# Projection weights as a float32r and a scaled float16 part in a fused attention block on one core

## The chip, the cores and the metric

The kernel runs on one core of one Trainium2 chip. The metric is the device time of one execution in microseconds (us), as the median of several runs. TensorE (PE) multiplies matrices into PSUM, VectorE (DVE) and ScalarE (ACT) read PSUM and SBUF, GpSimd (POOL) works on SBUF alone, SyncE (SP) issues most DMAs. Each engine takes its instructions in the order in which the program queued them.

## The reference

x has the shape (4, 512, 48, 48), so 4 batches, 512 channels and T = 2304 positions; 8 heads of 64 channels.

```python
hn = group_norm(x)                                  # 32 groups
qkv = einsum('oc,bchw->bohw', qkv_w, hn) + qkv_b    # float32, then cast to float16
w = softmax(einsum('bhct,bhcs->bhts', q * scale, k * scale))
a = einsum('bhts,bhcs->bhct', w, v).astype(float32) # a float16 result, widened
out = einsum('oc,bchw->bohw', proj_w, a) + proj_b
return x + out
```

The change concerns the last two lines: the projection of a with proj_w in float32, the bias proj_b, and the residual x.

## The kernel before

The program runs fast_path, which ends in a flag; if a test of its own has failed (a sum of exponentials out of range), general_path computes everything again.

fast_path goes through 16 pairs of heads (4 batches with 4 pairs each), and within a pair through 5 blocks of queries (four of 512 columns, one of 256). The work of a block is a stream of steps, three key tiles of two heads at a time: scores (L1066) on PE into one of three PSUM buffers, exponentials (L1073) on ACT into one of three p tiles, an add of that p tile to a running sum acc (L1122) on DVE, and the product with v (L1091) on PE into the only av buffer. At the end of a block, two joins (L1127) fold acc, a copy empties av (L1100), ones are multiplied with acc for the sums of the rows (L1150, also in the av buffer), and the sums go through SBUF and DRAM to be inverted and spread over partitions. GpSimd then writes the block's quotient to att in float16 (L1215).

Between the scores and the values of a step, fill (L1460) adds other work to PE's queue by a plan with fixed estimates of its cost: chains of matmuls for later pairs' q and k (L802) and v (L854), and the projection of the batch before. All these chains use one PSUM bank, ps_w, with a single buffer, so that a chain waits until the one before has been evacuated: q and k by L813, v by L862, the projection by L975, all on DVE. do_tasks adds statistics (L624) and normalization (L756) of the next batch on DVE.

The projection: the float16 result att of each pair is converted to float32r tiles at32 (att32, L940 on GpSimd and L942 on ACT). The weights of each of four channel chunks c are loaded during pair 0 and split (split_wproj, L566): whi is the weight rounded to float32r (L568), wlo the remainder, also in float32r (L569). proj_chain (L944) multiplies both parts with at32 and accumulates them: for each 128 output channels and 512 columns eight matmuls, in the order whi, wlo of c = 0, whi, wlo of c = 1 and so on. The evacuation (L975) adds the bias and the residual tile r in one operation; r, a part of x, is loaded two chains ahead (residual, L905). Batch 0 is projected during batch 1, batch 1 during batch 2, batch 2 and part of batch 3 during batch 3; for the last blocks of batch 3 the chain is cut in FIRST (three pairs, with the bias) and LAST (the fourth pair, L971, without it). In the tail `beyond` lets ACT copy a bank (L1592) and GpSimd add it to r.

fine (L593) holds the results of check_sums, which multiplies the outcome of each range test into it; at the end it is counted along with the tests of the last block (L1621 to L1644).

split_wproj is queued by put_run in pair 0, once for each chunk, between chains for q and k of pair 1.

Of the kernel before, what the change touches and what calls it, by code (L numbers as in the profile page):

```python
# [12 lines left out]
F32 = mybir.dt.float32  # L13
F32R = mybir.dt.float32r
F16 = mybir.dt.float16
I32 = mybir.dt.int32
AF = mybir.ActivationFunctionType
ALU = mybir.AluOpType
AX = mybir.AxisListType
# [3 lines left out]
B, C, T = 4, 512, 48 * 48  # L23
# [3 lines left out]
P = 128  # L27
NC = C // P
NPAIR = HEADS // 2
# [13 lines left out]
QB = 512  # L43
QBLOCKS = [(o, min(QB, T - o)) for o in range(0, T, QB)]
# [2 lines left out]


SUM_MIN, SUM_MAX = 256.0, 60000.0


IDLE = {"sync": 62, "scalar": 27, "gpsimd": 64, "tensor": 190}
# [418 lines left out]
def fast_path(  # L471
# [12 lines left out]
    nc = tc.nc  # L484

    RES = NC
    const = ctx.enter_context(tc.tile_pool(name="const", bufs=1))
# [37 lines left out]
    bproj = const.tile([P, NC], F32, name="bproj")  # L525
# [29 lines left out]


    whi = const.tile([P, NC, C], F32R, name="whi")
    wlo = const.tile([P, NC, C], F32R, name="wlo")

    wproj = {}  # L560

# [3 lines left out]

    def split_wproj(c):  # L566
        w = wproj.pop(c)
        nc.vector.tensor_copy(whi[:, c, :], w)  # L568
        nc.vector.tensor_tensor(  # L569
            wlo[:, c, :], w, whi[:, c, :].bitcast(F32), ALU.subtract  # L570
        )

    mhalf = const.tile([P, 2], F32, name="mhalf")
    nc.gpsimd.memset(mhalf, -0.5)
# [15 lines left out]
            channel_multiplier=sign,  # L590
        )

    fine = const.tile([P, 2 * QB // P], F32, name="fine")  # L593
    nc.gpsimd.memset(fine, 1.0)

# [2 lines left out]
    def chain_bank(name):  # L600
        if alone[0]:
            return ps_s.tile([P, 2, QB], F32, tag="ps", name=name)[:, 0, :]
        return ps_w.tile([P, QB], F32, tag="pw", name=name)
# [275 lines left out]
    atts, res, at32 = {}, {}, {}  # L879
# [9 lines left out]
    def rows_of(dram_tensor, b, j, chunks):  # L889
        o, n = QBLOCKS[j]  # L890
        found = dram_tensor[b, chunks[0] * P : (chunks[-1] + 1) * P, o : o + n]
        return found.rearrange("(m p) n -> p m n", p=P)
# [50 lines left out]

    def proj_chain(b, j, m, ps, pairs=range(NC)):  # L944
        n = QBLOCKS[j][1]
        steps = [(c, w) for c in pairs for w in (whi, wlo)]
        for i, (c, w) in enumerate(steps):
            nc.tensor.matmul(  # L948
                ps[:, :n],
                w[:, c, bass.ts(m, P)],  # L950
                at32[b, j, c],
                start=(i == 0),
                stop=(i == len(steps) - 1),
            )

    FIRST, LAST = range(NC - 1), range(NC - 1, NC)

    def proj_run(b, j, chunks, pairs=range(NC), bank=None):

        n = QBLOCKS[j][1]  # L960
        if bank is None:
            bank = chain_bank(f"pr_{b}_{j}_{chunks[0]}")
        places = [bank[:, i * n : (i + 1) * n] for i in range(len(chunks))]
        for m, ps in zip(chunks, places):
            proj_chain(b, j, m, ps, pairs)
        xt = res[b, j, chunks[0]]

        def evacuate():
            if pairs == LAST:
                ps = bank[:, : len(chunks) * n].rearrange("p (m n) -> p m n", n=n)  # L970
                nc.vector.tensor_tensor(xt, ps, xt, ALU.add)  # L971
            else:
                for i, m in enumerate(chunks):
                    bias = bproj[:, m : m + 1]
                    nc.vector.scalar_tensor_tensor(  # L975
                        xt[:, i], places[i], bias, xt[:, i], ALU.add, ALU.add
                    )

        def store(engine=nc.sync):
            engine.dma_start(rows_of(out, b, j, chunks), xt)  # L980

        return evacuate, store

    def proj_piece(b, j, chunks, pairs=range(NC), ahead=None):
        def run():
            evacuate, store = proj_run(b, j, chunks, pairs)
            evacuate()
            if pairs == LAST:
                finished.add((j, chunks[0]))

            if pairs != FIRST:
                loads.append((now[0] + 1, store))
            if ahead is not None:
                loads.append((now[0] + 1, ahead))

        return piece(QB / 290.0 * len(pairs) / NC, run, True, True)
# [320 lines left out]
    for b in range(B):  # L1317
        g = b * NPAIR
        old = b - 1
        if b == 0:  # L1320
            for j in range(NQ):
                if j < NC:
                    put_run(load_wproj, j)
                if j > 0:
                    put_run(split_wproj, j - 1)
                put_qk(g + 1, 1, (j,))
                put_qk(g + 1, 0, (j,))
            for block in SPARE:
                put_run(reload, *block)
# [183 lines left out]
    for n in range(end):  # L1513
# [34 lines left out]
        if n - BEHIND in soon:  # L1548
            g, j = stream[n - BEHIND][:2]
# [9 lines left out]
    g, b, j = NG - 1, B - 1, NQ - 1  # L1559
    n = QBLOCKS[j][1]  # L1560
# [21 lines left out]
    def last_run(k, bank=None):  # L1582
        return proj_run(b, *k, LAST, bank)

    def beyond(k, name, tag):
        bank = chain_bank(name)
        _, store = last_run(k, bank)
        t = xpool.tile([P, QB], F32, tag=tag, name=f"beyond_{name}")
        xt = res[b, k[0], k[1][0]].rearrange("p m n -> p (m n)")

        def copy():
            nc.scalar.copy(t, bank)  # L1592

        def finish():
            nc.gpsimd.tensor_tensor(xt, t, xt, ALU.add)  # L1595
            return store

        return copy, finish
# [4 lines left out]
    o = QBLOCKS[j][0]  # L1603
# [14 lines left out]
        copy, later = beyond(ahead[1], "ahead_1", "x1_3")  # L1618
        copy()

    every = fine.shape[1] + n  # L1621
    fines = work.tile([P, QB], F32, tag="rows", name="fines")[:, :every]
    nc.gpsimd.tensor_scalar(fines[:, :n], inv, 1.0 / SUM_MAX, None, ALU.is_ge)  # L1623
    ok = work.tile([P, QB], F32, tag="avx", name="ok")[:, :n]
    nc.gpsimd.tensor_scalar(ok, inv, 1.0 / SUM_MIN, None, ALU.is_le)  # L1625
    nc.gpsimd.tensor_tensor(fines[:, :n], fines[:, :n], ok, ALU.mult)  # L1626
    nc.gpsimd.tensor_copy(fines[:, n:], fine)  # L1627
    if len(ahead) > 1:
        store_ahead = later()

# [16 lines left out]
@with_exitstack  # L1647
def group_norm_attention(ctx: ExitStack, tc: tile.TileContext, *args):
    nc = tc.nc
    keep = ctx.enter_context(tc.tile_pool(name="keep", bufs=1))  # L1650
    flag = keep.tile([1, 1], I32, name="flag")

    kinds = mybir.EngineType
    engines = {kinds.PE, kinds.DVE, kinds.Pool, kinds.SP, kinds.Activation}
    with tc.manual_schedule(engines=engines):
        fast_path(tc, flag, *args)
    fails = nc.values_load(
        flag[0:1, 0:1],
        min_val=0,
        max_val=1,  # L1660
        skip_runtime_bounds_check_because="it is the result of a comparison",
    )
    with tc.If(fails > 0, label="fallback"):
        general_path(tc, *args)
# [37 lines left out]
```

## Time and profile before

| | us |
|---|---|
| median of 3 runs | 1597.47 |
| lowest and highest | 1597.33, 1597.59 |
| span of the profiled execution | 1595.6 |
| the runs' median less that span | 1.9 |

For the profiled execution the span, from its first to its last instruction, is the only time there is. A row of a group names the line, the engine, the operation, what it writes and reads with shapes, how often it ran, the busy us and the mean ns of one, and how long the engine was idle just before. A row of the timeline begins with its start and its length in us; "x6" merges six instructions of a kind. A row of windows has the length of the stretch, each engine's busy us with the number of instructions, the granted clock of TensorE, the share of DMA and GB/s. PE's matmuls are pipelined and their ends are modelled, so the distance from start to start says more than the length of one. PEld is the load of weights, which runs beside the matmul before it.

### The profile page before, as it was taken

Reading aid. Unit: us, or ns where it says so; the run is one execution under the profiler, and the core shown is the slowest. Engines: PE = TensorE matmul, PEld = TensorE weight load, DVE = VectorE, ACT = ScalarE, POOL = GpSimd, SP = SyncE. Lnnn points to the kernel's source line nnn. Section 1 sums busy time; section 2 is a strip of 40 time slices with the busy share of each in tenths; the row PEclk is TensorE's granted clock in tenths of the full one; section 3 lists DMA queues with packets and bytes.
Section 4 is the critical chain, followed back from the end, with each engine's and each line's share of the span. In section 5 each row is a group of like instructions: output and inputs, shape, how many; then the busy total and the mean of one; then the engine's idle time right before and its main releaser. Section 6 shows DMA issues by size and latency. Waiting matters only on the chain. (4 is left out here: it accounts for less than half of the span.)

```text
span 1595.6 us, 28731 instructions
## 1 busy us (share of the span) xinstructions
PE 1582.0 (99%) x11526; PEld 701.7 (44%) x11526; DVE 1140.2 (71%) x1302; ACT 1269.4 (80%) x1363; POOL 336.8 (21%) x463
## 2 busy tenths in 40 slices
PE   9999999999999999999999999999999999999997
PEld 3733434443333534545333354455533334434554
DVE  6267668876666678887666666888767676767776
ACT  4177777888888888888888888887878888888885
POOL 1001202222121222312112121222212121121232
PEclk9999999999999999999999999999999999999999
DMA  7002020000000024521000001353101000015424
GB/s 222 3 14 67 12 73 16 18 14 12 15 18 11 12 69 119 144 67 28 11 14 18 14 12 41 111 158 88 23 17 18 15 15 11 15 31 166 149 62 133
DMA packets 94896, 82.10 MB, mean 51 GB/s; under 512 B 50852, under 2 KB 60964, under 8 KB 94756
## 3 DMA queue, kind: packets, MB, share of 16 engines
q1 hardware_dynamic: 92724, 78.35, 18.1%
q8 instruction: 92, 1.51, 0.4%
q10 hardware_dynamic: 1904, 1.84, 0.4%
q14 instruction: 48, 0.39, 0.1%
q0 software_dynamic: 128, 0.01, 0.0%
HBM read 60.70 MB, written 19.17 MB: 50 GB/s over the span
## 5 line engine op out<-in xcount | busy, mean ns | idle before, releaser
L1073 ACT ACTIVATE p<-ps 128x1024 f16<-128x1024 f32 x1296 | 1233.5, 1025 | 299.1 <-PE ps L1066 296.3
L1122 DVE TENSOR_TENSOR acc<-acc,p 128x3072 f16<-128x3072 f16 x270 | 485.4, 1798 | 53.8 <-ACT p L1073 51.3
L802 PE MATMUL pqk<-x,wqkv 128*64 128x512 f32 (+1 forms) x2432 | 510.3, 549 | 0.1
L1091 PE MATMUL av<-p,v 128*64 128x512 f16 (+1 forms) x2880 | 360.6, 364 | 0.0
L1066 PE MATMUL ps<-q,k 64*128 64x512 f16 (+1 forms) x2880 | 355.8, 358 | 0.4 <-DVE v L862 0.2
L854 PE MATMUL pv<-wqkv,x 128*64 128x256 f32 x2304 | 267.6, 379 | 0.3 <-DVE v L862 0.3
L802 PEld LDWEIGHTS pqk<-x,wqkv 128*64 128x64 f32 x2432 | 168.5, 137 | 205.4 <-issue 155.9
L1188 POOL TENSOR_SCALAR in<-sums 128x8 f32<-128x8 f32 (+1 forms) x158 | 100.8, 638 | 712.4 <-DMA sums<-slx 705.8
L1066 PEld LDWEIGHTS <-k 64*128 64x128 f16 x2880 | 105.9, 94 | 287.2 <-issue 238.2
L1091 PEld LDWEIGHTS <-v 128*64 128x64 f16 x2880 | 131.2, 109 | 212.8 <-issue 168.1
L1215 POOL TENSOR_TENSOR att<-avx,ib 128x512 f16<-128x512 f32 (+1 forms) x78 | 133.1, 1706 | 422.9 <-DMA ib<-row 373.7
L854 PEld LDWEIGHTS pv<-wqkv,x 128*64 128x64 f32 x2304 | 166.3, 137 | 81.3 <-DVE v L862 0.8
L1122 DVE TENSOR_TENSOR acc<-p,p 128x3072 f16<-128x3072 f16 x79 | 138.1, 1748 | 0.0
L948 PE MATMUL pr<-a,whi 128*128 128x512 f32 (+1 forms) x311 | 121.8, 399 | 0.1
L1127 DVE TENSOR_TENSOR acc<-acc 128x1024 f16<-128x1024 f16 x156 | 114.7, 735 | 3.3
L948 PE MATMUL pr<-a,wlo 128*128 128x512 f32 (+1 forms) x311 | 113.5, 372 | 0.0
L813 DVE TENSOR_SCALAR q<-pqk,bqkv 128x512 f16<-128x512 f32 (+1 forms) x77 | 53.5, 694 | 76.0 <-PE pqk L802 75.5
L813 DVE TENSOR_SCALAR k<-pqk,bqkv 128x512 f16<-128x512 f32 (+1 forms) x75 | 52.2, 695 | 77.7 <-PE pqk L802 77.5
L862 DVE TENSOR_TENSOR v<-pv,bv 128x512 f16<-128x512 f32 x72 | 49.7, 690 | 79.6 <-PE pv L854 79.5
L1166 DVE COPY slx<-sl 128x512 f32<-128x512 f32 (+1 forms) x79 | 50.6, 641 | 64.1 <-PE sl L1150 64.1
L975 DVE SCALAR_TENSOR_TENSOR r<-pr,bproj,r 128x512 f32<-128x512 f32 (+1 forms) x80 | 54.9, 695 | 41.3 <-PE pr L948 36.6
L1100 DVE COPY avx<-av 128x512 f32<-128x512 f32 (+1 forms) x79 | 50.6, 640 | 36.4 <-PE av L1091 36.1
(124 smaller groups left out, 506.7 us busy)
## 6 DMA issues: line engine op xcount, KB each, us to landing
r<-x_dram SPq DMA_DIRECT2D x72, 256.0 KB, 3.6
out_dram<-r SPq DMA_DIRECT2D x69, 256.0 KB, 2.4
ib<-row SPq DMA_DIRECT2D x126, 128.0 KB, 3.1
x<-x_dram SPq DMA_DIRECT2D x62, 256.0 KB, 3.9
x<-x_dram SPq DMA_DIRECT2D x16, 128.0 KB, 4.8
sums<-slx SPq DMA_DIRECT2D x128, 2.0 KB, 2.1
ib<-row SPq DMA_DIRECT2D x30, 64.0 KB, 3.0
wqkv<-qkv_wT_dram SPq DMA_DIRECT2D x2, 768.0 KB, 6.9
```

The costliest lines, as they stand in the source:

```text
L802: nc.tensor.matmul(pw[0][lo : lo + D, :n], wqkv[:, c, w0 + lo : w0 + lo + D], hn[b, c, j], start=(c == 0), stop=(c == NC - 1),)
L813: nc.vector.tensor_scalar(qk[g][part][:, o : o + n], pw[0][:, :n], bqkv[:, col : col + 1], SCALE, ALU.add, ALU.mult,)
L854: nc.tensor.matmul(pw[0][lo : lo + D, a, :], hn[b, c, i * P // QB][:, at + lo : at + lo + D], wqkv[:, c, 2 * C + half * C // 2 :][:, : C / ...
L948: nc.tensor.matmul(ps[:, :n], w[:, c, bass.ts(m, P)], at32[b, j, c], start=(i == 0), stop=(i == len(steps) - 1),)
L975: nc.vector.scalar_tensor_tensor(xt[:, i], places[i], bias, xt[:, i], ALU.add, ALU.add)
L1066: nc.tensor.matmul(ps[:, h, a * n : (a + 1) * n], kt[rows, bass.ts(i, P)], qt[rows, o : o + n], start=True, stop=True,)
L1073: nc.scalar.activation(pt[:, r], ps, AF.Exp)
L1091: nc.tensor.matmul(av[0][lo : lo + D, :n], vv[b, pr // 2][:, i, pr % 2 * P + lo : pr % 2 * P + lo + D], pt[:, r, h, a * n : (a + 1) * n], ...
L1122: nc.vector.tensor_tensor(t, before, pt, ALU.add)
L1127: nc.vector.tensor_tensor(t[:, 0], t[:, 0], t[:, r], ALU.add)
L1188: nc.gpsimd.tensor_scalar(t, sm, limit, None, op)
L1215: nc.gpsimd.tensor_tensor(atts[g][:, o : o + n], avx.pop((g, j))[:, :n], ibs.pop((g, j))[:, :n], ALU.mult,)
```

## The change

The weight is scaled by 2^26 when it is split. whi is the scaled weight rounded to float32r; the remainder is cast to float16 as wlo, and whether that cast was exact is tested on the chip: GpSimd subtracts wlo from the remainder and compares with zero, DVE takes the minimum into split_ok, four new columns of the tile that held fine. At the end these are counted with the other tests. In a chain, wlo comes ahead of whi and multiplies att itself, in float16; whi multiplies at32 as before. The scale is taken out at the evacuation (DOWN). The bias is no longer added there but to the residual tile, in operations of its own that are queued ahead of the chain.

```diff
+UP = 2.0**26
+DOWN = 1.0 / UP
...
-    wlo = const.tile([P, NC, C], F32R, name="wlo")
+    wlo = const.tile([P, NC, C], F16, name="wlo")
...
     def split_wproj(c):
         w = wproj.pop(c)
-        nc.vector.tensor_copy(whi[:, c, :], w)
-        nc.vector.tensor_tensor(
-            wlo[:, c, :], w, whi[:, c, :].bitcast(F32), ALU.subtract
+        nc.vector.tensor_scalar(whi[:, c, :], w, UP, None, ALU.mult)
+        nc.vector.scalar_tensor_tensor(
+            w, w, UP, whi[:, c, :].bitcast(F32), ALU.mult, ALU.subtract
         )
+        nc.vector.tensor_copy(wlo[:, c, :], w)
+        nc.gpsimd.tensor_tensor(w, w, wlo[:, c, :], ALU.subtract)
+        nc.gpsimd.tensor_scalar(w, w, 0.0, None, ALU.is_equal)
+        nc.vector.tensor_reduce(split_ok[:, c : c + 1], w, AX.X, ALU.min)
...
-    fine = const.tile([P, 2 * QB // P], F32, name="fine")
-    nc.gpsimd.memset(fine, 1.0)
+    tests = const.tile([P, 2 * QB // P + NC], F32, name="tests")
+    nc.gpsimd.memset(tests, 1.0)
+    fine, split_ok = tests[:, : 2 * QB // P], tests[:, 2 * QB // P :]
...
     def proj_chain(b, j, m, ps, pairs=range(NC)):
         n = QBLOCKS[j][1]
-        steps = [(c, w) for c in pairs for w in (whi, wlo)]
-        for i, (c, w) in enumerate(steps):
+        o = QBLOCKS[j][0]
+        steps = [
+            s
+            for c in pairs
+            for s in (
+                (wlo[:, c], atts[b * NPAIR + c][:, o : o + n]),
+                (whi[:, c], at32[b, j, c]),
+            )
+        ]
+        for i, (w, a) in enumerate(steps):
             nc.tensor.matmul(
                 ps[:, :n],
-                w[:, c, bass.ts(m, P)],
-                at32[b, j, c],
+                w[:, bass.ts(m, P)],
+                a,
...
+        xt = res[b, j, chunks[0]]
+        if pairs != LAST:
+            for i, m in enumerate(chunks):
+                nc.vector.tensor_scalar(
+                    xt[:, i], xt[:, i], bproj[:, m : m + 1], None, ALU.add
+                )
         for m, ps in zip(chunks, places):
             proj_chain(b, j, m, ps, pairs)
-        xt = res[b, j, chunks[0]]

         def evacuate():
-            if pairs == LAST:
-                ps = bank[:, : len(chunks) * n].rearrange("p (m n) -> p m n", n=n)
-                nc.vector.tensor_tensor(xt, ps, xt, ALU.add)
-            else:
-                for i, m in enumerate(chunks):
-                    bias = bproj[:, m : m + 1]
-                    nc.vector.scalar_tensor_tensor(
-                        xt[:, i], places[i], bias, xt[:, i], ALU.add, ALU.add
-                    )
+            ps = bank[:, : len(chunks) * n].rearrange("p (m n) -> p m n", n=n)
+            nc.vector.scalar_tensor_tensor(xt, ps, DOWN, xt, ALU.mult, ALU.add)
...
-            nc.scalar.copy(t, bank)
+            nc.scalar.mul(t, bank, DOWN)
...
-    every = fine.shape[1] + n
+    every = tests.shape[1] + n
...
-    nc.gpsimd.tensor_copy(fines[:, n:], fine)
+    nc.gpsimd.tensor_copy(fines[:, n:], tests)
```

## The prediction

> **What bounds the kernel now.** I read the engines' line of the page first, then the groups by shape, then busy time by window for the stretches that hold projection work, and last the timeline around the lines the change touches.
>
> ```profile
> span 1595.6 us, 28731 instructions
> PE 1582.0 (99%) x11526; PEld 701.7 (44%) x11526; DVE 1140.2 (71%) x1302; ACT 1269.4 (80%) x1363; POOL 336.8 (21%) x463
> ```
> TensorE (PE) has work for 99% of the span, so time saved on it is time saved, and any wait put in front of it is time lost. The other engines have slack on average. The average hides three stretches in which the projection chains of batches 0, 1 and 2 run:
>
> ```profile
> 628.90:686.00 57.10, 57.10 (x356) 32.10 (x356) 51.55 (x74) 47.97 (x56) 19.03 (x23) 1.00 0.56 158
> 1035.50:1092.20 56.70, 56.70 (x316) 30.10 (x314) 50.94 (x71) 48.38 (x57) 12.16 (x18) 1.00 0.56 161
> 1445.40:1502.00 56.60, 56.60 (x353) 32.04 (x352) 40.55 (x44) 49.95 (x61) 16.84 (x25) 1.00 0.65 198
> ```
> Columns: length, then busy us of PE, weight loads, VectorE (DVE), ACT, POOL. In the first two VectorE is busy for 51.55 of 57.10 and 50.94 of 56.70 us (90%), because it also normalizes the next batch there; in the third for 40.55 (72%).
>
> **Saving on TensorE.** Each 512-wide chain is eight matmuls (four pairs of whi and wlo). One chain:
>
> ```profile
> 629.03 0.50 PE L948 MATMUL pr<-a,whi 128*128 128x512 f32 x1
> 629.36 0.39 PE L948 MATMUL pr<-a,wlo 128*128 128x512 f32 x1
> ...
> 630.76 0.39 PE L948 MATMUL pr<-a,wlo 128*128 128x512 f32 x1
> 631.08 0.82 PE L1066 MATMUL ps<-q,k 64*128 64x512 f16 x6
> ```
> From the second to the eighth start, 629.36 to 630.76 us, six steps take 1.40 us: 0.233 us each. The first step takes 0.33 us: the first weight load of a chain isn't hidden. The groups show it over all chains:
>
> ```profile
> L948 PE MATMUL pr<-a,whi 128*128 128x512 f32 x251 | 106.4, 424 | 0.1
> L948 PE MATMUL pr<-a,wlo 128*128 128x512 f32 x251 | 99.0, 394 | 0.0
> ```
> (106.4 - 99.0) = 7.4 us is what the open first loads cost in the 512-wide chains. The change does two things here. It puts wlo first, with float16 weights, and it runs half the matmuls with float16 on both sides. The rows nearest to that are the warm-up matmuls, float16 with 128x128 weights and 512 columns:
>
> ```profile
> 1.52 4.95 PE L1405 MATMUL idle<-busy 128*128 128x512 f16 x16 [1.52 <-DVE busy L1401]
> 8.85 1.02 PE L1405 MATMUL idle_again<-busy 128*128 128x512 f16 x4
> L1405 PEld LDWEIGHTS <-busy x20: 95/98/181, 1.5 to 9.3; 128*128 128x128 f16 x20
> L948 PEld LDWEIGHTS pr<-a,wlo x311: 187/188/192, 629.1 to 1577.7; 128*128 128x128 f32 x156
> ```
> Four take 1.02 us, of which the last one's own duration is 0.38: 0.64 over three steps, 0.214 us a step against 0.233. So a wlo matmul saves 0.019 us; for the 251 of the group 4.8 us. The float16 load takes 98 ns against 188: 90 ns of the 100 ns that the first load leaves open go, 0.9 x 7.4 = 6.7 us. Together 11.5 us; the half-width chains may add up to 1 us (estimate, half the columns and fewer of them). If the load saves nothing, 4.8 us stay; that is the low end. The Trainium skill, page "TensorE: Matmul & The Clock Gate", section on weight-path perf modes, says that 128 weights that aren't FP32 are read in four parallel chunks, and its load formula gives 107 ns for 128 columns; by these, as an estimate, the saving per chain would be 80 ns instead of 90 and the sum of first loads 6 us. The traced loads go the same way, and I keep the rows.
>
> Of the 11.5 us, each of the first two windows holds 16 chains of 64 + 64 matmuls: 64 x 0.019 + 16 x 0.09 = 2.7 us. That leaves 11.5 - 5.4 = 6.1 us for batches 2 and 3 and the tail.
>
> **Cost on VectorE: the bias.** Each 512-wide chain gets a 128x512 float32 tensor_scalar in SBUF. It stands in VectorE's queue behind the previous work and ahead of the evacuation, which still waits for the chain. Its residual tile is loaded two chains ahead, and the evacuation waited for the same load before, so no new DMA wait. The nearest row is the float32 cast of the split (next fence): 0.42 us, and 84.35 to 84.80, 0.45 us, until the next starts. The evacuation itself stays what it was, one operand instead of another. In the first window VectorE then needs 51.55 + 16 x 0.45 = 58.75 us, while TensorE needs 57.1 - 2.7 = 54.4. VectorE becomes the bound of that window; the single ps_w bank makes TensorE wait for each late evacuation, so the lag can't be carried along. I take 58.75: +1.65 us, and the same in the second window: +3.3 together. Bounds: -2.7 each, if the new operations fit into idle time; +3.3 each, if VectorE also keeps a third of its 5.5 idle us. In the third window 40.55 + 7.2 = 47.8 stays under 53.9: no higher share than the first window has today, so the saving stays.
>
> **Cost in the splits.** split_wproj runs four times in pair 0. Today it is two VectorE operations. After it is four, then a wait for two GpSimd operations on the same tile, then a reduction, all ahead of everything queued later on VectorE: the adds of L1122, the evacuations of L813, the av copy of L1100. TensorE waits for the last two, since ps_w and ps_av have one buffer each.
>
> ```profile
> 84.35 0.42 DVE L568 CAST whi<-wproj 128x512 fp32r<-128x512 f32 x1
> 84.80 0.69 DVE L569 TENSOR_TENSOR wlo<-wproj,whi 128x512 fp32r<-128x512 f32 x1
> 85.41 3.61 DVE L1122 TENSOR_TENSOR acc<-acc,p 128x3072 f16<-128x3072 f16 x2
> 90.16 0.75 DVE L813 TENSOR_SCALAR k<-pqk,bqkv 128x512 f16<-128x512 f32 x1 [1.14 <-PE pqk L802]
> 91.46 3.60 PE L802 MATMUL pqk<-x,wqkv 128*64 128x512 f32 x16
> ...
> 96.84 1.75 DVE L1122 TENSOR_TENSOR acc<-acc,p 128x3072 f16<-128x3072 f16 x1
> 98.62 1.42 DVE L1127 TENSOR_TENSOR acc<-acc 128x1024 f16<-128x1024 f16 x2
> 99.96 0.68 DVE L1100 COPY avx<-av 128x512 f32<-128x512 f32 x1
> 101.59 0.75 DVE L813 TENSOR_SCALAR k<-pqk,bqkv 128x512 f16<-128x512 f32 x1 [0.95 <-PE pqk L802]
> 102.46 1.90 PE L802 MATMUL pqk<-x,wqkv 128*64 128x512 f32 x8
> ...
> 110.03 1.75 DVE L1122 TENSOR_TENSOR acc<-acc,p 128x3072 f16<-128x3072 f16 x1
> 113.26 0.75 DVE L813 TENSOR_SCALAR k<-pqk,bqkv 128x512 f16<-128x512 f32 x1 [1.48 <-PE pqk L802]
> 114.56 1.88 PE L802 MATMUL pqk<-x,wqkv 128*64 128x512 f32 x8
> ...
> 121.47 0.69 DVE L1127 TENSOR_TENSOR acc<-acc 128x1024 f16<-128x1024 f16 x1
> 122.07 0.68 DVE L1100 COPY avx<-av 128x512 f32<-128x512 f32 x1
> 122.98 0.48 DVE L813 TENSOR_SCALAR k<-pqk,bqkv 128x256 f16<-128x256 f32 x1 [0.23 <-PE pqk L802]
> 123.86 1.89 PE L802 MATMUL pqk<-x,wqkv 128*64 128x256 f32 x16
> ```
> For GpSimd's two operations the nearest rows are:
>
> ```profile
> L1215 POOL TENSOR_TENSOR att<-avx,ib 128x512 f16<-128x512 f32 x63 | 113.4, 1801 | 332.4 <-DMA ib<-row 301.1 <-DVE acc L1122 21.5 <-DVE q L813 5.2
> L940 POOL CAST a<-att 128x512 fp32r<-128x512 f16 x32 | 23.3, 751 | 43.8 <-PE pr L948 36.5 <-PE pqk L802 7.3
> L1177 POOL TENSOR_TENSOR att<-avx,inv 128x512 f16<-128x512 f32 x1 | 1.3, 1269 | 9.4 <-DVE inv L1176 9.4
> L1625 POOL TENSOR_SCALAR ok<-inv 128x256 f32<-128x256 f32 x1 | 0.9, 851 | 0.0
> ```
> The subtraction: 1.27 us (alone) to 1.80 (mean). The comparison: twice 0.85 = 1.70 us, as it is the same kind on twice the columns; at least the 0.75 of the cast. I take 1.27 and 1.70, since VectorE stands still meanwhile. The delay of all that follows: 0.45 + 0.61 (as now) + 0.42 (float16 copy) + 0.1 + 1.27 + 1.70 + 0.1 + 0.61 (reduction, like L569 one element at a time) = 5.26, less today's 1.06: 4.2 us; 3.25 to 4.7 at the bounds (0.1 for a semaphore is an estimate). Followed through the rows:
> - First: adds from 89.6, done 93.2, evacuation done 93.95. TensorE wanted the bank at 91.46: 2.5 us lost.
> - Second: add from 101.05, joins, copy and evacuation back to back end at 105.45; wanted 102.46: 3.0 us.
> - Third: 114.23 + 1.68 + 0.75 = 116.65; wanted 114.56: 2.1 us.
> - Fourth: 125.67 + 0.62 + 0.62 + 0.48 = 127.4; wanted 123.86: 3.5 us.
> Sum 11.1 us, 7.3 to 13.2 at the bounds. TensorE is full afterwards too, so nothing is won back.
>
> Priced at nothing: the shorter wait for att32 in the tail (wlo no longer needs the converted tile, whi still does), the scaled ACT copy, four more columns in the final count, all beside work of the same engines; without that cover some tenths of a us. atts tiles are now read until the last projection of their batch, which ended before GpSimd's next write to that buffer.
>
> **Sum.** +11.1 (splits) + 3.3 (two windows) - 6.1 (rest) = +8.3 us. The profiled span 1595.6 becomes 1603.9; the runs' median lies 1.9 us above the span (1597.47), so 1605.8 us.
>
> **Rivals.**
> *VectorE keeps up (faster).* If the reduction stands later in VectorE's queue than its place in the code, behind the adds, GpSimd's time is covered and a split delays the queue by 0.42 + 0.61 = 1.0 us; only the fourth, which has about 0.7 us of slack, reaches TensorE, with 0.3 us. With the bias inside idle time in both windows the time is 1597.5 + 0.3 - 11.5 = 1586.3. It decides from a delay below about 1.7 us a split. For: VectorE is idle for 29% of the span and waits for TensorE ahead of many evacuations (0.95 to 1.48 us in the rows above). Against: the order of the queue is the order of the code, and the tile of the reduction is written by GpSimd. With the splits at 7.3 and the windows at -5.4 it is 1597.5 + 7.3 - 11.5 = 1593.3.
> *A draw.* Splits at 7.3 us, windows at 0, rest -6.1: 1598.7.
> *Changing types costs TensorE.* A change of the array's shape costs 0.32 (630.76 to 631.08) instead of 0.233 us. If each change between float16 and float32r did the same, 2 x 251 changes x 0.09 would be +45 us, about 1650. Against it stands a change of type at one shape:
>
> ```profile
> 79.81 0.38 PE L1091 MATMUL av<-p,v 128*64 128x512 f16 x2
> 80.03 3.60 PE L802 MATMUL pqk<-x,wqkv 128*64 128x512 f32 x16
> ```
> 0.22 us, no more than a step within float16.
> *The clock falls in the four stalls.* The first sixteen warm-up matmuls took (4.95 - 0.38) / 15 = 0.305 us a step, later ones 0.214: 1.4 us lost after idleness. Four times that is +5.5: 1611. The rule behind it is in the Trainium skill, "TensorE: Matmul & The Clock Gate", Part 1 (the HAM clock gate): about 3.4 us without work halve the clock. My stalls are mostly shorter than that.
> *The test fails.* If the remainder isn't exact in float16, the flag sends the kernel through general_path, a second whole computation behind the first: over 3000 us (estimate, twice the present time).
>
> **How the numbers follow.** Forecast case 0.60; VectorE keeps up in one of its two forms 0.20; draw 0.13; clock 0.04; types 0.02; test 0.01. About 0.2% (3.2 us) can be told from no change: faster 0.20, same 0.13, slower 0.67. The range: low is the sum with all cheap ends, 1593, drawn to 1591 for the half-width chains; high is 13.2 + 6.6 - 3 (the load saves nothing) = +16.8, 1614.
>
> **What would show it.** Right: L1066, L802 and L1150 with 2 to 3.5 us of idle time ahead of them four times before 130 us, released by L813 or L1100, and a VectorE gap that ends at the reduction, released by GpSimd; the two windows 1 to 3 us longer, VectorE near full; wlo loads of about 98 ns, the first step of a chain near 0.24 us. Wrong: no TensorE idle time before 130 us; windows shorter than 55 us; whi steps that grow above 0.24 us behind a float16 matmul.

## The result and the profile after

The changed kernel takes 1621.49 us (median of 5 runs, 1621.1 to 1623.22) against 1597.33 (5 runs, 1597.29 to 1597.59): ratio 1.0152, interval 1.0141 to 1.0163, so 24.2 us slower. The forecast was 1605.8, the range ended at 1614: the sign was right, the size a third of what came. The profiled execution has a span of 1619.5 us against 1595.6, +23.9.

The engines' line of the changed kernel, to be read against the first fence of the prediction:

```profile
span 1619.5 us, 28813 instructions
PE 1581.0 (98%) x11526; PEld 666.2 (41%) x11526; DVE 1178.0 (73%) x1382; ACT 1269.6 (78%) x1363; POOL 347.5 (21%) x471
```
TensorE is busy for as long as before (1581.0 against 1582.0), so the 23.9 us are nearly all time in which it waits. (Two things cancel in the busy time, both shown below: 3.4 us that TensorE loses at half clock, and what the shorter chains save.) VectorE has 38 us more work, in 80 more instructions.

Where they lie is read from the groups of projection matmuls in each stage (duration min/median/max in ns, then first and last start in us), here batch 0's:

```profile
L966 PE MATMUL pr<-a,whi x64: 577/578/589, 643.9 to 704.0; 128*128 128x512 f32 x64
```
A table of these rows for all kernels that matter (us; "to" is the last start of a stage's projection matmuls; batches 0 and 1 with their 512-wide chains only):

| kernel | batch 0 | batch 1 | batches 2, 3 | span |
|---|---|---|---|---|
| before | 629.0 to 685.6 | 1035.6 to 1091.9 | 1445.5 to 1577.9 | 1595.6 |
| after | 643.9 to 704.0 | 1054.4 to 1113.1 | 1467.3 to 1601.1 | 1619.5 |
| no_test | 629.2 to 689.0 | 1039.5 to 1098.6 | 1452.8 to 1586.7 | 1605.3 |
| no_bias | 644.7 to 699.1 | 1049.2 to 1104.2 | 1457.9 to 1585.8 | 1604.7 |
| f16_plain | 629.2 to 683.5 | 1033.7 to 1088.2 | 1442.0 to 1570.0 | 1588.0 |
| grouped | 629.1 to 683.4 | 1033.2 to 1088.3 | 1441.7 to 1568.7 | 1586.9 |
| bias_alone | 629.0 to 688.9 | 1038.8 to 1097.6 | 1451.5 to 1586.3 | 1604.8 |

From the first start of one stage to the first of the next, after less before: +14.9 us ahead of batch 0's projection (the splits), +3.9 from there to batch 1's, +3.0 to batch 2's, +2.1 to the end. The prediction had +11.1, +1.65, +1.65 and -6.1.

**The splits.** The timeline of the changed kernel around the first one, VectorE and GpSimd, and the TensorE chain that waits (the bracket is idle time and what ended it):

```profile
85.83 0.43 DVE L577 CAST wlo<-wproj 128x512 f16<-128x512 f32 x1
86.33 1.16 POOL L578 TENSOR_TENSOR wproj<-wproj,wlo 128x512 f32<-128x512 f32 x1 [59.22 <-DVE wlo L577]
87.58 1.51 POOL L579 TENSOR_SCALAR wproj<-wproj 128x512 f32<-128x512 f32 x1
89.12 0.69 DVE L580 TENSOR_REDUCE tests<-wproj 128x1 f32<-128x512 f32 x1 [2.87 <-POOL wproj L579]
...
93.26 0.74 DVE L823 TENSOR_SCALAR k<-pqk,bqkv 128x512 f16<-128x512 f32 x1
...
94.06 3.69 PE L812 MATMUL pqk<-x,wqkv 128*64 128x512 f32 x16 [2.13 <-DVE k L823]
```
VectorE stands for 2.87 us at the reduction, and the evacuation two rows below releases the bank 2.13 us late: the step as forecast. The second split ends in a wait of 2.38 us for the copy of av (L1116) and one of 0.25 for the evacuation. The third and fourth end in these TensorE rows:

```profile
122.83 3.54 PE L812 MATMUL pqk<-x,wqkv 128*64 128x512 f32 x8 [2.48 <-DVE k L823]
...
136.79 0.64 PE L1166 MATMUL sl<-acc,ones 128*64 128x512 f16 x2 [3.10 <-DVE avx L1116]
137.18 3.41 PE L812 MATMUL pqk<-x,wqkv 128*64 128x256 f32 x16
```
Eight L812 matmuls take 1.88 us elsewhere, here 3.54; sixteen of half width took 1.89 before, here 3.41. The windows of the changed kernel show why (length, busy us of PE, PEld, DVE, ACT, POOL, then the granted clock):

```profile
92.40:95.81 3.41, 1.75 (x8) 0.76 (x10) 3.27 (x3) 2.03 (x3) 0.00 (x0) 1.00 0.00 0
...
119.71:123.12 3.41, 0.93 (x8) 0.34 (x6) 3.41 (x4) 2.33 (x3) 0.79 (x1) 0.99 0.00 0
123.12:126.53 3.41, 3.41 (x10) 0.75 (x8) 3.27 (x3) 0.00 (x0) 0.00 (x0) 0.50 0.00 0
...
133.36:136.77 3.41, 0.33 (x4) 0.10 (x1) 1.92 (x4) 2.79 (x3) 1.46 (x1) 1.00 0.00 0
136.77:140.19 3.42, 3.40 (x16) 2.08 (x17) 2.71 (x3) 0.00 (x0) 0.00 (x0) 0.51 0.05 6
```
Twice TensorE runs at half clock for 3.41 us, just after a wait, and loses some 1.7 us each time (3.54 - 1.88 and 3.41 - 1.89 + 0.64 - 0.41).

**The chains.** One chain of the changed kernel, TensorE's timeline, and the groups of all:

```profile
1470.79 0.39 PE L966 MATMUL pr<-att,wlo 128*128 128x512 f16 x1
1470.83 0.59 PE L966 MATMUL pr<-a,whi 128*128 128x512 f32 x1
1471.25 0.39 PE L966 MATMUL pr<-att,wlo 128*128 128x512 f16 x1
...
1472.74 0.82 PE L1082 MATMUL ps<-q,k 64*128 64x512 f16 x6
```
```profile
L966 PE MATMUL pr<-a,whi 128*128 128x512 f32 x251 | 124.2, 582 | 0.0
L966 PE MATMUL pr<-att,wlo 128*128 128x512 f16 x251 | 97.5, 389 | 14.9 <-DVE r L993 14.5
```
From wlo to wlo 0.46 us, nearly as much as two float32r steps took (2 x 0.233): next to nothing is won inside a pair. The chain lasts 1.95 us (1470.79 to 1472.74) against 2.05 (629.03 to 631.08), 0.10 less, about the open first load. And ahead of the wlo matmuls there are now 14.5 us of waiting for the evacuation L993, where before the groups of the chains show 0.1 and 0.0.

**VectorE.** Its two groups in the changed kernel:

```profile
L985 DVE TENSOR_SCALAR r<-r,bproj 128x512 f32<-128x512 f32 x64 | 38.0, 593 | 3.7 <-DMA r<-x_dram 3.7
L993 DVE SCALAR_TENSOR_TENSOR r<-pr,r 128x512 f32<-128x512 f32 x75 | 51.8, 691 | 17.1 <-PE pr L966 11.3
```
The bias operation takes 593 ns on average, not 450, and it waits for the residual's DMA, which the prediction had excluded. Fifteen of the 64 take over 0.6 us, 14.7 us together, and each of these lies beside a conversion (L950) or a quotient (L1231) on GpSimd; the other 49 take 0.475 us on average. The windows that answer to the three of the prediction, and a fourth stretch behind them, with the same stretch before the change above it:

```profile
643.80:704.40 60.60, 55.35 (x354) 23.03 (x352) 57.98 (x89) 47.91 (x55) 17.11 (x23) 1.00 0.53 147
1054.30:1113.60 59.30, 55.29 (x314) 21.23 (x312) 57.23 (x86) 48.30 (x57) 15.02 (x18) 1.00 0.52 152
1467.20:1523.60 56.40, 54.65 (x352) 22.54 (x350) 47.38 (x58) 49.70 (x60) 18.09 (x25) 1.00 0.65 194
```
```profile
1502.00:1540.00 38.00, 38.00 (x243) 19.80 (x242) 30.86 (x34) 33.31 (x38) 11.25 (x14) 1.00 0.16 41
1523.60:1563.00 39.40, 37.24 (x244) 16.11 (x242) 36.51 (x48) 33.33 (x38) 12.27 (x15) 1.00 0.17 47
```
In the first two VectorE is busy for 96%: it is the bound, as forecast. In the third it is busy for 84% only, and TensorE still lacks 1.75 us: nearly the same matmuls take 56.40 us where they took 56.60. In the stretch behind it, which holds projection chains too, VectorE goes from 81% to 93%, and TensorE, which never stopped there, lacks 2.16 us. The prediction did not look at that stretch. One wait from the third window and two from behind it:

```profile
1513.49 0.49 DVE L985 TENSOR_SCALAR r<-r,bproj 128x512 f32<-128x512 f32 x1 [1.00 <-DMA r<-x_dram]
...
1514.83 0.38 PE L966 MATMUL pr<-att,wlo 128*128 128x512 f16 x1 [1.09 <-DVE r L993]
...
1550.05 1.69 POOL L1231 TENSOR_TENSOR att<-avx,ib 128x512 f16<-128x512 f32 x1 [2.18 <-DMA ib<-row]
1550.53 1.49 DVE L985 TENSOR_SCALAR r<-r,bproj 128x512 f32<-128x512 f32 x1
...
1552.87 0.38 PE L966 MATMUL pr<-att,wlo 128*128 128x512 f16 x1 [0.81 <-DVE r L993]
...
1569.55 0.48 DVE L985 TENSOR_SCALAR r<-r,bproj 128x512 f32<-128x512 f32 x1 [1.48 <-DMA r<-x_dram]
...
1570.88 0.38 PE L966 MATMUL pr<-att,wlo 128*128 128x512 f16 x1 [1.26 <-DVE r L993]
```
A wait of 1.00 or 1.48 us in front of the bias, or a bias operation of 1.49 us beside GpSimd, holds back the evacuation behind it, and TensorE stands for 1.09, 1.26 and 0.81 us.

### The profile page after: what moved, and what is told of

Read it like the earlier page. It is cut to its first block, busy times and chain, and to the rows that moved or that the text cites. A ratio compares the mean times of both kernels' runs of the same rounds, so it can differ in the third digit from the quotient of the medians.

```text
span 1619.5 us, 28813 instructions
## 1 busy us (share of the span) xinstructions
PE 1581.0 (98%) x11526; PEld 666.2 (41%) x11526; DVE 1178.0 (73%) x1382; ACT 1269.6 (78%) x1363; POOL 347.5 (21%) x471
## 5 line engine op out<-in xcount | busy, mean ns | idle before, releaser
L812 PE MATMUL pqk<-x,wqkv 128*64 128x512 f32 (+1 forms) x2432 | 513.5, 552 | 5.0 <-DVE k L823 4.9
L812 PEld LDWEIGHTS pqk<-x,wqkv 128*64 128x64 f32 x2432 | 169.8, 138 | 211.8 <-issue 157.0
L1231 POOL TENSOR_TENSOR att<-avx,ib 128x512 f16<-128x512 f32 (+1 forms) x78 | 128.5, 1648 | 417.8 <-DMA ib<-row 344.7
L966 PE MATMUL pr<-a,whi 128*128 128x512 f32 (+1 forms) x311 | 139.8, 540 | 0.0
L966 PE MATMUL pr<-att,wlo 128*128 128x512 f16 (+1 forms) x311 | 112.5, 368 | 14.9 <-DVE r L993 14.5
L1116 DVE COPY avx<-av 128x512 f32<-128x512 f32 (+1 forms) x79 | 50.5, 640 | 35.6 <-PE av L1107 35.3
L1205 POOL TENSOR_TENSOR tests<-tests,in 128x8 f32<-128x8 f32 (+1 forms) x158 | 69.3, 439 | 13.2
## 6 DMA issues: line engine op xcount, KB each, us to landing
ib<-row SPq DMA_DIRECT2D x126, 128.0 KB, 3.1
x<-x_dram SPq DMA_DIRECT2D x16, 128.0 KB, 4.8
```

The costliest lines, as they stand in the source:

```text
L812: nc.tensor.matmul(pw[0][lo : lo + D, :n], wqkv[:, c, w0 + lo : w0 + lo + D], hn[b, c, j], start=(c == 0), stop=(c == NC - 1),)
L966: nc.tensor.matmul(ps[:, :n], w[:, bass.ts(m, P)], a, start=(i == 0), stop=(i == len(steps) - 1),)
L1205: nc.gpsimd.tensor_tensor(ok, ok, t, ALU.mult)
L1231: nc.gpsimd.tensor_tensor(atts[g][:, o : o + n], avx.pop((g, j))[:, :n], ibs.pop((g, j))[:, :n], ALU.mult,)
```

## The experiments

The theory was that the 24 us are three things: the test's waits in the splits (with the clock behind them), the bias on VectorE in all stages, and a float16 saving that is only the open first load. Its rivals were a changed type that costs TensorE itself, a loss that stays when one part is taken out, and, for the clock, that it would fall whatever the length of the wait. Every ratio stands against the kernel before, with its interval.

**1. Without the test.**
```diff
         nc.vector.tensor_copy(wlo[:, c, :], w)
-        nc.gpsimd.tensor_tensor(w, w, wlo[:, c, :], ALU.subtract)
-        nc.gpsimd.tensor_scalar(w, w, 0.0, None, ALU.is_equal)
-        nc.vector.tensor_reduce(split_ok[:, c : c + 1], w, AX.X, ALU.min)
```


> Leaves out the test of the split: GpSimd's two operations and the reduction behind them (the flag's columns stay at one). Theory W (waits in VectorE's queue, with the clock falling after two of them): the 14.5 us that the changed kernel has lost by 130 us into the span go, the rest of its loss stays: 1621.5 - 14.5 = 1607, and no stretch at half clock before 200 us. Rival (the loss before 130 us comes from the heavier split operations on VectorE, not from the wait): at most 2 us are won, 1619 or more.

Measured: 1607.61 us, ratio 1.0067 (1.005 to 1.0084), 13.9 us less than the whole change. TensorE in the windows of this kernel:

```profile
80.00:145.00 65.00, 65.00 (x408) 22.16 (x406) 47.26 (x52) 49.27 (x53) 5.72 (x10) 1.00 0.15 46
```
It never stops there, the clock stays at 1.00, and batch 0's first chain starts at 629.2 (before 629.0, after 643.9). The loss ahead of it is the test's.

**2. Without the bias operations.**
```diff
         xt = res[b, j, chunks[0]]
-        if pairs != LAST:
-            for i, m in enumerate(chunks):
-                nc.vector.tensor_scalar(
-                    xt[:, i], xt[:, i], bproj[:, m : m + 1], None, ALU.add
-                )
```


> Leaves out the bias operations of the chains (the bias isn't added). Theory W: VectorE is behind in the projection stretches only because of them; then each 512-wide chain keeps the 0.10 us that it is shorter on TensorE, about 8 us over all, and the first 14.5 us of loss stay: 1597.4 + 14.5 - 8 = 1604. Rival (evacuations are late for another reason, such as the alternation of types on TensorE): 1615 or more, with TensorE still waiting for evacuations about 14 us in sum.

Measured: 1606.36 us, ratio 1.0056 (1.0039 to 1.0073), 15.1 us less than the whole change. Its waits have this row in place of 14.5 us:

```profile
PE pr L966 <- DVE r L988: 0.8, 2, 0.5
```
The stages shrink from 60.1, 58.7 and 133.8 us to 54.4, 55.0 and 127.9: 5.7, 3.7 and 5.9. The third one is the longest, with twice the chains of the first. Its first part is the prediction's third window:

```profile
1457.80:1512.20 54.40, 54.40 (x352) 22.31 (x350) 41.17 (x44) 49.46 (x59) 16.68 (x24) 1.00 0.69 203
```
The same 352 matmuls took 56.40 us with the bias, so 2.0 of the 5.9 us fall into that window and 3.9 behind it.

**3 and 4. The float16 part alone, in pairs and in groups.** Both start from the kernel before: wlo in float16, not scaled and not tested (the remainder is rounded), times att itself, with the bias in the evacuation. In f16_plain the pairs are those of the change:
```diff
-    wlo = const.tile([P, NC, C], F32R, name="wlo")
+    wlo = const.tile([P, NC, C], F16, name="wlo")
...
-        steps = [(c, w) for c in pairs for w in (whi, wlo)]
+        steps = [
+            s
+            for c in pairs
+            for s in (
+                (wlo[:, c], atts[b * NPAIR + c][:, o : o + n]),
+                (whi[:, c], at32[b, j, c]),
+            )
+        ]
```
In grouped, the four float16 matmuls of a chain come first:
```diff
-        steps = [(c, w) for c in pairs for w in (whi, wlo)]
+        steps = [
+            (wlo[:, c], atts[b * NPAIR + c][:, o : o + n]) for c in pairs
+        ] + [(whi[:, c], at32[b, j, c]) for c in pairs]
```


> The kernel before with one part of the change alone: wlo in float16, unscaled, ahead of whi and multiplying att; bias in the evacuation and no test, as before (the remainder is rounded to float16). Theory W: the shorter chains are a gain of 0.10 us each, 64 + 8 of them and more starts in batch 3: 1597.4 - 8 = 1589, with pairs of matmuls still at 0.464 us. Rival (two types in one chain cost as much as they save): 1597 or more.

> As f16_plain, but a chain runs its four float16 matmuls first and its four float32r ones behind them, one change of type instead of seven. If a change of type costs what the faster float16 step would save (a pair takes 0.464 us where 0.214 + 0.233 = 0.447 was expected), the float16 steps show 0.214 us and the time is another 4 to 5 us lower: 1585. If the float16 step is no faster than float32r in this place whatever stands ahead of it: the same as f16_plain, 1589.

Measured: f16_plain 1590.29 us, 0.9957 (0.994 to 0.9973); grouped 1588.52, 0.9943 (0.9927 to 0.996). So the float16 part is worth 7.1 us, not 11.5. In grouped, the timeline and the groups:

```profile
1445.09 1.04 PE L951 MATMUL pr<-att,wlo 128*128 128x512 f16 x4
1445.77 1.28 PE L951 MATMUL pr<-a,whi 128*128 128x512 f32 x4
1446.98 0.82 PE L1069 MATMUL ps<-q,k 64*128 64x512 f16 x6
```
```profile
L951 PE MATMUL pr<-a,whi 128*128 128x512 f32 x251 | 82.2, 445 | 0.1
L951 PE MATMUL pr<-att,wlo 128*128 128x512 f16 x251 | 65.7, 381 | 1.8 <-DVE r L978 1.8
```
A chain takes 1.89 us here (1445.09 to 1446.98). Four wlo take 1.04 us with the last one's 0.381: 0.22 a step, the warm-up's pace that the prediction used. It is there in groups and not in alternation. Yet the time falls by 1.8 us only, where 4 to 5 were expected, and the two intervals overlap. A chain of f16_plain takes 1.94 us (629.17 to 631.11), so at 0.05 us a chain some 3 us could be won over 64 chains (an estimate from these rows), and the waits for the evacuation took 1.8 us against 0.6.

**5. The same with whi first.** Against f16_plain:
```diff
-                (wlo[:, c], atts[b * NPAIR + c][:, o : o + n]),
                 (whi[:, c], at32[b, j, c]),
+                (wlo[:, c], atts[b * NPAIR + c][:, o : o + n]),
```

> As f16_plain, with whi ahead of wlo in each pair. If the gain of f16_plain is the open first weight load of a chain (float16 98 ns instead of 188), it is lost: 0.10 us for each of some 80 chain starts, 1597 to 1598.5. If the gain comes from the pairs themselves, or from the product that no longer waits for at32: the same as f16_plain, 1590.

Measured: 1596.29 us (10 runs), ratio 0.9993 (0.9983 to 1.0003). With the float32r load again at the head of the chain all but 1.0 us of the gain is gone. The open first load was 6.0 of the 7.1 us; that is the prediction's term of 6.7 us, confirmed, and its term of 4.8 us, refuted. A wait of the first product for at32 is no rival to that: neither in this run nor before the change (0.1 us of idle time in sum) did a matmul of a chain stand idle for it, and their weight loads waited for it for 1.2 us in sum in both.

**6. Half of the test.** GpSimd's subtraction and the reduction stay (into a tile that nothing reads), the comparison goes.
```diff
         nc.gpsimd.tensor_tensor(w, w, wlo[:, c, :], ALU.subtract)
-        nc.gpsimd.tensor_scalar(w, w, 0.0, None, ALU.is_equal)
-        nc.vector.tensor_reduce(split_ok[:, c : c + 1], w, AX.X, ALU.min)
+        nc.vector.tensor_reduce(unused[:, c : c + 1], w, AX.X, ALU.min)
```


> The changed kernel without GpSimd's comparison: VectorE still waits for the subtraction and still reduces (into a tile that nothing reads; the test's columns stay at one). The wait is 1.5 us shorter in each split. If the loss is wait plus a clock that falls after waits of about 2.5 to 3 us, four waits of 2.4, 2.9, 2.5 and 3.1 us on TensorE become 0.9, 1.4, 1.0 and 1.6 (4.9 in sum) and no stretch runs at half clock: 14.5 - 4.9 = 9.6 us less, 1612. If the clock falls whatever the length of the wait: 3.6 us more, 1615.5.

Measured: 1610.38 us, ratio 1.0081 (1.0064 to 1.0098), no window at half clock before the last 10 us (mean granted clock 0.999 against 0.996), batch 0's first chain at 633.5: 4.5 us late. The total is 1.6 us below the expectation's 1612, within the interval. With waits of at most 1.5 us the clock holds; of the test's 14.9 us, the comparison and the clock behind it are 10.4.

**7. The whole test, reduction two steps later.**
```diff
-        nc.vector.tensor_reduce(split_ok[:, c : c + 1], w, AX.X, ALU.min)
+        def reduce():
+            nc.vector.tensor_reduce(split_ok[:, c : c + 1], w, AX.X, ALU.min)
+        loads.append((now[0] + 2, reduce))
```


> The changed kernel with the whole test, but the reduction queued two steps later on VectorE, behind the adds and the evacuation of that time. If it is the place in the queue that costs, GpSimd's 2.7 us are covered and the time is that without the test plus little: 1608 to 1610, with TensorE never idle for over 1 us before 130 us. Rival (GpSimd's work on the tile slows VectorE's own work, wherever the reduction stands): 1612 or more.

Measured: 1609.53 us, ratio 1.0076 (1.0059 to 1.0093). The total met the expectation, the account did not: TensorE should hardly have waited, and it waits up to 1.71 us. In its timeline the first reduction is still early:

```profile
88.68 1.51 POOL L579 TENSOR_SCALAR wproj<-wproj 128x512 f32<-128x512 f32 x1
90.23 0.69 DVE L582 TENSOR_REDUCE tests<-wproj 128x1 f32<-128x512 f32 x1 [2.65 <-POOL wproj L579]
...
93.30 3.69 PE L816 MATMUL pqk<-x,wqkv 128*64 128x512 f32 x16 [1.71 <-DVE k L827]
```
Two steps were not enough (GpSimd's subtraction took 2.60 us in three of the four splits, where it ran beside VectorE's adds, against 1.16). Three were: experiment 10 holds the same test with the reduction three steps later, and its first chain of batch 0 starts at 629.7, 0.7 us late instead of 14.9.

**8. The bias alone.** The kernel before, with the bias in operations of its own ahead of the chains, and a plain add as the evacuation; no float16, no test.
```diff
+        if pairs != LAST:
+            for i, m in enumerate(chunks):
+                nc.vector.tensor_scalar(
+                    xt[:, i], xt[:, i], bproj[:, m : m + 1], None, ALU.add
+                )
         for m, ps in zip(chunks, places):
             proj_chain(b, j, m, ps, pairs)
...
+            ps = bank[:, : len(chunks) * n].rearrange("p (m n) -> p m n", n=n)
+            nc.vector.tensor_tensor(xt, ps, xt, ALU.add)
```

> The kernel before with one other part of the change alone: the bias in operations of its own ahead of the chain, the evacuation a plain add. In the changed kernel leaving them out won 15 us. If VectorE's lack of time makes the loss, it appears here too, smaller by what the longer chains leave (0.1 us a chain): 1597.4 + 7 = 1604, at least 1602. If it needs the shorter float16 chains to show: 1599 or less.

Measured: 1606.96 us, ratio 1.0062 (1.0045 to 1.0079): 9.6 us for the operations by themselves. The run no_test, which has the same operations and the float16 part as well, took 1607.61: with the bias in front of the chains, the 7.1 us of the float16 part do not show at all. This fits the 15.1 us that the same operations cost in the changed kernel. The stages grow to 59.9, 58.8 and 134.8 us, from 56.6, 56.3 and 132.4.

**9. The bias behind an evacuation.** As 8, with the bias of the next chain queued behind the evacuation of this one (add_bias holds the operation of 8, once for each chain).
```diff
             evacuate()
+            k = proj_list.index((j, chunks)) + 1
+            if pairs == range(NC) and k < len(proj_list):
+                if (b, proj_list[k][0], proj_list[k][1][0]) in res:
+                    add_bias(b, *proj_list[k])
```

> As bias_alone, but the bias of the next chain is added behind the evacuation of this one instead of ahead of its own, where the residual is there already. The same work on VectorE in another place. If it is the amount of work in the projection stretches that costs, the time stays at 1605 to 1607; if it is the place right ahead of the evacuation, half or more of the 9.6 us goes: 1602 or less.

Measured: 1637.97 us, ratio 1.0253 (1.0236 to 1.027). Both expectations missed. The waits of this kernel:

```profile
DVE r L966 <- DMA r<-x_dram: 49.7, 29, 3.5
...
PE pr L948 <- DVE r L984: 31.1, 25, 3.2
```
Moved ahead by one chain, the operation stands in VectorE's queue before the residual has landed (29 waits, up to 3.5 us), and all behind it stands too. That early request is a cost of its own. Part of the loss is also the clock, which the trace has at half for 10.2 us in the projection stretches (from 677.7 and 1063.4 us).

**10. The bias on GpSimd**, with grouped chains and the reduction three steps later.
```diff
-                nc.vector.tensor_scalar(
+                nc.gpsimd.tensor_scalar(
                     xt[:, i], xt[:, i], bproj[:, m : m + 1], None, ALU.add
```


> The whole change (scaled split, exact float16 remainder and its test) with three edits: the reduction queued three steps later, the four float16 matmuls of a chain first, and the bias added by GpSimd. If VectorE's queue was all that cost, the gain of grouped (8.9 us) shows, less about 2 us for the heavier split: 1590 to 1592. If GpSimd's 64 operations of about 1.5 us hold up its divisions and conversions, which the chains wait for: 1598 or more.

Measured: 1642.93 us, ratio 1.0284 (1.0267 to 1.0302). GpSimd is busy for 21% of the span in the changed kernel, yet:

```profile
L984 POOL TENSOR_SCALAR r<-r,bproj 128x512 f32<-128x512 f32 x64 | 114.4, 1793 | 28.0 <-DMA r<-x_dram 15.9 <-DVE slx L1181 4.6 <-DVE r L992 4.6
```
```profile
DVE r L992 <- POOL r L984: 78.5, 37, 4.5
PE pr L965 <- DVE r L992: 44.9, 34, 3.2
```
1.79 us for one operation, three times VectorE's, and in a chain: VectorE waits 78.5 us for GpSimd, TensorE 44.9 us for VectorE. The clock adds to it: six times before the last 10 us, for 3.41 us each, the trace has it at half, which is some 10 of the 45 us (an estimate, half of that time).

**11 and 12. Half and twice the bias.** The whole change, with the bias added to half of the columns, and added twice.
```diff
+                h = n // 2
                 nc.vector.tensor_scalar(
-                    xt[:, i], xt[:, i], bproj[:, m : m + 1], None, ALU.add
+                    xt[:, i, :h], xt[:, i, :h], bproj[:, m : m + 1], None, ALU.add
```
```diff
-            for i, m in enumerate(chunks):
+            for i, m in [*enumerate(chunks), *enumerate(chunks)]:
```

> The changed kernel with the bias operations on half the columns of each residual tile (the other half gets no bias). If the amount of VectorE work makes the loss, 64 operations of about 0.34 instead of 0.59 us take 16 us off its queue and about half of the 15 us goes: 1612 to 1616. If the loss is the waiting that such an operation does whatever its size (for the residual's load, for GpSimd): 1618 or more.

> The changed kernel with each bias operation done twice (the bias is added twice). If the amount makes the loss, 38 us more VectorE work go into stretches that have no idle time left, nearly all of it shows: 1645 to 1660. If the waiting makes it, the second operation has nothing left to wait for: 1625 to 1635.

Measured: 1615.71 us (1.0113, 1.0096 to 1.013) and 1645.77 us (1.0304, 1.0287 to 1.0321). With 2 and the change itself this is a series: busy time of the bias 0, 32.3 (447 ns for 256 columns), 42.7 and 80.2 us; time 1606.4, 1615.7, 1621.5 and 1645.8. One us of it costs 0.29 us up to the half, 0.56 from there to the whole and 0.65 beyond: first VectorE's idle time takes up most, then TensorE pays for two thirds. The traces of none and of half have three stretches at half clock before 150 us, the two others two; counted from the first projection chain on, where none of the four has one before its last 10 us, the spans are 960.0, 969.7, 975.6 and 1000.3 us and say the same. In the last kernel the waits read

```profile
PE pr L966 <- DVE r L993: 36.2, 46, 1.9
```

## Why the prediction was wrong

**What bounds the kernel**: right. TensorE's busy time stayed (1581.0 against 1582.0 us), and it stands idle for 24.9 us more in a span that is 23.9 us longer.

**Saving on TensorE (-11.5)**: the step "a wlo matmul saves 0.019 us; for the 251 of the group 4.8 us" failed. The pace came from float16 behind float16; the change alternates. The pair takes 0.46 us whichever part leads (experiments 3 and 5), and the faster step shows only in groups (4). The first load's 6.7 us were right (7.1 measured, 1.0 with whi first). The fence on a change of type at one shape, quoted against the third rival, shows the way from float16 to float32 (x and wqkv are float32, not float32r), with weights of 64 columns. The way back is in the same trace, behind the eight matmuls of L802 that start at 102.46:

```profile
104.18 0.83 PE L1091 MATMUL av<-p,v 128*64 128x512 f16 x6
```
That is 1.72 us for the eight, and eight more of them in one chain add as much (sixteen from 91.46 to 94.99, eight from 88.22 to 90.04: 1.71 apart), so there it cost nothing either. But float16 in turn with float32r, on weights of 128 columns, was in no row that the prediction had, and that is what the change runs. Why the alternation keeps the slower pace stays open.

**Cost in the splits (+11.1)**: the waits were right. TensorE stood for 2.1, 2.6, 2.5 and 3.1 us, 10.3 together; the single splits were forecast at 2.5, 3.0, 2.1 and 3.5. (The 0.1 us for a semaphore, an estimate of the prediction, was 0.03 to 0.09 us in the rows of the first split.) What failed is "The clock falls in the four stalls", put at 4 in 100 because "My stalls are mostly shorter than that". It fell after two of the four and cost 3.4 us; with the waits that is 13.7 of the 14.9 us. The length of a wait is the wrong thing to look at. In the windows above, the stretches at half clock begin 13.65 us apart, four times 3.413, and in the run without the bias operations they begin at 106.9, 124.0 and 137.6 us: five and four times 3.413. On that grid the clock halves after a stretch in which TensorE had work for 0.93 or 0.33 of 3.41 us and stays after one with 1.75. The kernel with half the bias brackets it from below:

```profile
90.77:94.18 3.41, 1.28 (x10) 0.48 (x10) 3.31 (x4) 2.85 (x3) 0.00 (x0) 1.00 0.00 0
94.18:97.59 3.41, 3.41 (x10) 1.24 (x8) 1.25 (x1) 0.01 (x1) 0.00 (x0) 0.50 0.00 0
```
The Trainium skill, page "TensorE: Matmul & The Clock Gate", Part 1 (The HAM clock gate), has a free-running window of 3413 ns; these runs agree. It lets the clock fall after a whole idle window; here 2.48 us without work, in a window with 0.93 us of work, did it. The measurement decides. The same wait, 2.38 us in the second split, was followed by a fall in the run without the bias operations and not in the changed kernel: there it left 1.32 us of work in one stretch of the grid, here it lay across two, with 2.33 and 1.86 (windows from 102.64 and 106.05 us).

```profile
103.51:106.92 3.41, 1.32 (x10) 0.32 (x7) 3.34 (x4) 2.26 (x3) 0.00 (x0) 1.00 0.00 0
```
So a wait of 2.5 us may or may not cost 1.7 more, depending on where it lies on a grid that moves from run to run.

**Cost on VectorE (+3.3)**: the mechanism was right, its size was not. VectorE became the bound of the two windows, and the 54.4 us forecast for the first one without the bias are near the 54.9 of no_bias (54.4 from first to last start, and half a us at the ends, as before has 57.1 and 56.6). But the bias operation takes 0.593 us, not 0.45; "no new DMA wait" was wrong (4.4 us in six waits, the longest 1.5); and with those the first window came to 60.6 us where 58.75 was forecast. Without the bias operations the evacuation waited for that load once, for 1.3 us; the operation ahead of the chain asks for it some 2 us earlier, by the length of a chain. (Two figures of that paragraph are slightly off: the second window gives 50.94 + 7.2 = 58.1, so +1.4, and the upper bound, 1.65 and a third of 5.5, is +3.5 a window.)

**"In the third window ... the saving stays" (-6.1)** was the largest miss: +2.1 us, 8.2 off. Two steps failed. In the window itself VectorE's share, 84%, is below that of the first window before the change (90%), and still 2.0 us went to the bias: TensorE waits for single late evacuations, and a mean over 56 us says nothing of a DMA wait of 1.0 us ahead of one of them. And the saving was carried on through the rest of batch 3 on the strength of that one window; there VectorE was at 81% before and at 93% after, and the bias cost 3.9 us. The float16 saving in the whole stage was 4.4 us (132.4 to 128.0 in f16_plain), not 6.1.

Put together from the runs: -7.1 for the float16 part, +13.9 for the test, +15.1 for the bias make 21.9 of the measured 24.2 us. The rest of 2.3 us is within what the single differences are uncertain by (each interval is about 2.7 us to either side) and was not taken apart. One part of it is known: in its trace the run without the bias operations starts batch 0's projection 0.8 us later than the changed kernel, with a third stretch at half clock, which hides as much of the bias's cost.

**The other rivals**: a draw and a faster kernel fell. Changing types did not cost TensorE 45 us. The second computation did not run, as the span shows.

The fastest version run is grouped, 1588.5 us, with the remainder rounded to float16 and no test. Whether it beats f16_plain is open. A version with the exact, tested remainder, the reduction three steps later and the bias left in the evacuation would, by the 0.7 us that those splits cost in experiment 10, lie near it; it was not run.

## What to carry to other kernels

A test or a sum that another engine has to finish belongs as many steps behind in the queue as that engine needs, for the one that waits holds up all behind it (here 14.9 us against 0.7). An operation that is queued ahead of a chain asks for its inputs earlier than the one it relieves, and where a buffer is single its worst case counts, not the mean share of busy time in one window; and every stretch with such chains has to be looked at, not the first of them. A pace taken from repeated matmuls of one type holds for such a repetition only: order the chain so, or measure the alternation.

## What the hardware showed that was not expected

- The half-clock stretches lie on a grid of 3.413 us and, before the last 10 us of a kernel, last 3.41 us each (one, in experiment 9, twice that: 2.19 us of work in its first half did not raise the clock again). In the traces of all kernels here, a stretch of the grid at full clock with up to 1.39 us of TensorE work out of 3.41 was followed by one, and none with 1.6 or more was. Between the two it went either way: 1.46 and 1.52 were followed by one (experiment 10), 1.43 (experiment 10) and 1.48 (experiment 12) were not.
- A float16 matmul of 512 columns between float32r ones gains next to nothing (0.46 us a pair against 0.466); grouped, four of them run at 0.22 us a step.
- The bias operation on VectorE, 128x512 float32 in SBUF, took 0.41 to 1.50 us. All 15 over 0.6 us lay beside GpSimd's conversion (L950) or quotient (L1231), both with 512 columns; of the 49 others 14 lay beside a GpSimd operation, 12 of them beside one on a small tile (128x2 to 128x8). The slowing is seen in the other direction too: GpSimd's subtraction took 1.16 us while VectorE waited and 2.60 us beside its adds. No run separates this from other causes.
- A like operation took 1.79 us on GpSimd.
